# Layer 2's first upper product formed ahead from layer 1's sums and rows, with x2 made beside hop 1

## The chip, the cores and the metric

One Trainium2 chip, one core. The metric is the device time of one execution in microseconds (us), lower is better; several executions of a kernel are timed, and one more is profiled.

## The reference, cut to what matters

Four graph layers over N = 3327 nodes with 64 features and one dense-stored, sparsely filled adjacency matrix `adj`; each layer is added to its input and normalised. The change lies between layer 1 and layer 2:

```python
# layer 1: hyperbolic attention; m_i = sum_j v_ij * rows_j, then a chain of scalars per node,
# whose end is  x2 = layernorm(x1 + layer1(x1))
x = _layernorm(x + _L1_gnn_ref(x, adj, L1_gnn_att_W, L1_gnn_att_b), axis=-1)
# layer 2: two hops
for k in range(HOP):
    agg = adj @ x
    x = jnp.tanh(jnp.concatenate([agg, x], axis=1) @ W[k])
```

The concatenation makes each hop `tanh(adj @ (x @ W_top) + x @ W_bottom)`. For each node, x2 is a combination `alpha * m + beta * xc` of layer 1's sums m and of the centred input rows xc, with two scalars alpha and beta that come out of the chain.

## The kernel before, in words

Nodes are padded to 26 blocks of 128 (`NB`), which lie in pairs: a `[128, 26, 64]` tile holds one block's rows per slot, and the transposed form `[128, 1664]` stacks a pair's 64 features twice. Chunks of 416 columns (`CW`) cut the 1664 (`HALF`) into four. The adjacency is held transposed in HBM, one block of 128 rows being 1664 KB.

**Layer 1** (`near_sphere`, from L973) runs 104 tiles. For each: TensorE products (L1053), VectorE and ScalarE work (L1065, L1066, L1074), and sums of `v` over nodes on TensorE (`acc`, L1086). The four sums are copied to `mT` (L1094). `gather` is called for each tile in turn; after the third last tile TensorE takes six early products with `all_m` (L1264), and ScalarE reads them after the last but one (L1269, L1273). GpSimd multiplies mT and ljT for the sums of products `p` (L1259 for half of mT, L1277 for a quarter). Here `ljT[0]` holds layer 1's rows, transposed.

**`blocks_ahead`** (L1657) then opens the buffers for the adjacency blocks of layer 2 (`strm`, four of them; `late`, two), in memory that layer 1's tiles had, and issues their loads on SyncE (all by L209, in `block`): blocks 0 to 3 (`at_l`) and two that stay for both hops (`kept`, blocks 20 and 21). Blocks 22 to 25 have been kept since the start. SyncE's order is the planner's; those of TensorE, ScalarE and VectorE in these stages are written out by hand (`manual_schedule`), GpSimd's only in layer 1's loop.

**`near_end`** (L1286) is the chain of scalars, 26 per partition: three sums per node (`p`, `q` and the last feature `t`) from products with `all_m` (L1340) and `but_last` (L1350), some forty small VectorE operations with a tanh (L1392) and two roots by ScalarE (L1422, in `rsqrt2`, with one Newton step each), idle matmuls that keep TensorE awake (`awake`, L1326), and the centred weights of layer 3 (`centred_weights`, L301). Then x2 = al * m + bx, bx = be * xc: GpSimd (L1454) and ScalarE (L1457) make bx, VectorE the rest (L1463 to L1467).

**`layers`** (L309) begins with hop 1 (k = 0). `turned` transposes a group of x2 (L345, L349), `top` multiplies it by the upper weights and copies the product to `hw` = `lj` (L355, L391), `bottom` multiplies by the lower weights into the accumulators (L394), and `add` adds one adjacency block: 8 products of 128x416 by halves (L403). The order of the blocks is 0 to 3, 25, 4 to 7, 24, 8 to 11, 23, 12 to 15, 22, 16 to 19, and at the end 20 and 21 chunk by chunk (`chunk_end`, L475), with the tanh (L478). New blocks are loaded into `strm` (`at_l`) and `more` (`bt_l`, two buffers) as TensorE frees them. Hop 2 takes the same way, beginning with the last six blocks that hop 1 loaded; layer 3 follows.

Hop 1's head, in short, interleaves the making of hw with the first two blocks:

```python
turned(0); turned(1); top(0, nc.scalar.copy); turned(2); top(1)
for c in range(CPH): add(c, order[0])
turned(3); top(2); turned(4); top(3)
for c in range(CPH): add(c, order[1])
top(4)
for c in range(CPH): bottom(c)
```

Of the kernel before, what the change touches and what calls it, by code (L numbers as in the profile page):

```python
# [10 lines left out]
F32 = mybir.dt.float32  # L11
# [3 lines left out]
AF = mybir.ActivationFunctionType  # L15
# [8 lines left out]
D = 64  # L24
# [49 lines left out]
def kernel(  # L74
# [234 lines left out]
    def layers(ctx, x2, x3, kept, ready, ahead_ctx, strm):  # L309
# [67 lines left out]
        with tc.tile_pool(name="l2p", bufs=2, space=PSUM, reuse_waits="tile") as l2p:  # L377
            for k in range(2):
# [49 lines left out]
                if k == 0:  # L428
# [20 lines left out]
                else:  # L449
# [13 lines left out]
                for i, jb in enumerate(order):  # L463
# [6 lines left out]
                    for c in range(CPH):  # L470
                        add(c, jb)
                    if k and jb in held and len(held) == 2:
                        for q in range(AHEAD + 3):
                            masks(q)
# [384 lines left out]
    with tc.tile_pool(name="l1", bufs=1) as l1:  # L859

        def l1_stat(name):
            return l1.tile([P, NB], F32, name=name)

        aa, g1, ga, xn, rxn, gs, gs2, gk, lpn = (
            l1_stat(name) for name in ("aa", "g1", "ga", "xn", "rxn", "gs", "gs2", "gk", "lpn")
# [107 lines left out]
        def near_sphere(mT, xm, sq_e, t_e):  # L973
# [3 lines left out]
            with tc.tile_pool(name="n1", bufs=1, reuse_waits="tile") as n1, tc.tile_pool(  # L977
# [10 lines left out]
                ljT = [n1.tile([P, HALF], F32, name=f"ljT_{k}") for k in range(2)]  # L988
# [206 lines left out]
                with tc.manual_schedule(  # L1195
# [80 lines left out]
                    of = slice(2 * CW, 3 * CW)  # L1276
                    nc.gpsimd.tensor_tensor(xm[:, of], mT[:, of], ljT[0][:, of], ALU.mult)  # L1277
                    layer_3_constants()
# [5 lines left out]
                    vec(xn, aa, rxn, ALU.mult)  # L1284

        def near_end(mT, xm, sq_e, t_e, x2):  # L1286
# [3 lines left out]
            with tc.tile_pool(name="l1e", bufs=1) as l1e, tc.tile_pool(  # L1290
                name="l1t", bufs=1, space=PSUM
            ) as l1t, tc.tile_pool(name="l1m", bufs=5, space=PSUM) as l1m:

                prod = l1e.tile([P, NB, D], F32, name="prod_xm")
                sqm = l1e.tile([P, NB, D], F32, name="prod_mm")
# [14 lines left out]
                def both(a, scalar, b, tag, op0, op1):  # L1310
# [5 lines left out]
                    engines={mybir.EngineType.PE, mybir.EngineType.Activation, mybir.EngineType.DVE}  # L1316
                )
                in_order.__enter__()
                gss = of(mul, gs, s, "gss")
                gks = both(gk, -2.0, s, "gks", mul, mul)  # L1320
                aav = lin(aa, 1.0 / D, LN_EPS, "aav")
                idle = l1t.tile([P, 512], F32, name="idle_e")

                def awake(t):

                    nc.tensor.matmul(  # L1326
                        idle[:NB, :], t, xc[:, :8].rearrange("p n d -> p (n d)"),
                        start=True, stop=True,
                    )

                gt = st("gt")
                p, q = st("p"), st("q")
                nc.vector.tensor_reduce(q[:, :12], sq_e, axis=AX.X, op=add)
                pms = {}

                def both_products(g, n):

                    pm = l1m.tile([P, 3, P + 2], F32, tag="pm", name=f"pm_{g}")[:, :n]
                    for k in range(n):
                        nc.tensor.matmul(  # L1340
                            pm[:, k], mT[:, (g + k) * P : (g + k + 1) * P], all_m,
                            start=True, stop=True,
                        )
                    pms[g] = pm

                for g, n in threes[2:]:
                    both_products(g, n)
                pe = l1t.tile([P, 9, 2], F32, name="pe")
                for k in range(9):
                    nc.tensor.matmul(  # L1350
                        pe[:, k], xm[:, k * P : (k + 1) * P], but_last, start=True, stop=True
                    )
                for g, n in threes[:2]:
                    both_products(g, n)
                for g, n in threes[2:]:
                    m = pms[g][:, :, :P].rearrange("p n (h d) -> p n h d", h=2)
                    nc.scalar.activation(by_half(sqm)[:, g : g + n], m, AF.Square)
                    if g > 6:
                        vec(by_half(prod)[:, g : g + n], m, by_half(xc)[:, g : g + n], mul)
                vec(gt[:, :12], t_e, gk[:, :12], mul)  # L1360
                for g, n in threes[2:]:
                    sl = slice(2 * g, 2 * (g + n))
# [4 lines left out]
                nc.vector.tensor_reduce(p[:, 18:], prod[:, 18:], axis=AX.X, op=add)  # L1367
                nc.vector.tensor_reduce(q[:, 12:], sqm[:, 12:], axis=AX.X, op=add)
                nc.vector.tensor_copy(p[:, :18], pe.rearrange("p n h -> p (n h)"))

                k = of(mul, p, gks, "k")
                vec(k, k, gt, add)
                gp = of(mul, p, gss, "gp")
                vec(p, p, s, mul)
# [7 lines left out]
                awake(u2)  # L1382
                centred_weights(l1t)
# [6 lines left out]
                awake(th)  # L1390
                arg, th = th, st("tanh")
                nc.scalar.activation(th, arg, AF.Tanh, scale=-1.0)  # L1392
# [10 lines left out]
                al = of(mul, ca, gs, "al")  # L1403
                vec(be, be, ck, sub)
                alp = of(mul, al, p, "alp")
                bea = of(mul, be, aa, "bea")
                al2 = of(mul, al, al, "al2")
                n2 = both(alp, 2.0, bea, "n2", mul, add)
                vec(al2, al2, q, mul)
                vec(n2, n2, be, mul)  # L1410
                vec(alp, alp, bea, add)
                vec(n2, n2, al2, add)
                awake(n2)
                root = lin(n2, MIN_NORM * MIN_NORM, None, "root", ALU.max, ALU.bypass)
                dn = lin(y2, 1.0, None, "dn", add, ALU.bypass)
                stt(dn, uy, 2.0, dn, op0=mul, op1=add)
                sca(dn, dn, MIN_NORM, None, ALU.max)

                def rsqrt2(v, tag):

                    r0 = st(f"{tag}_r")
                    nc.scalar.activation(r0, v, AF.Sqrt)  # L1422
                    awake(v)
                    nc.vector.reciprocal(r0, r0)
                    t = of(mul, v, r0, f"{tag}_t")
                    vec(t, t, r0, mul)
                    stt(t, t, -3.0, r0, op0=add, op1=mul)
                    return t


                r0 = st("rdn")
                nc.vector.reciprocal(r0, dn)
                on = rsqrt2(root, "on")
                f = both(on, -0.5 * MAX_NORM, r0, "f", mul, ALU.min)
                vec(n2, n2, f, mul)
                vec(al, al, f, mul)
                stt(n2, alp, 2.0, n2, op0=mul, op1=add)
                vec(be, be, f, mul)
                vec(n2, n2, f, mul)
                sca(be, be, 1.0, None, add)  # L1440
                stt(n2, n2, 1.0 / D, aav, op0=mul, op1=add)
                vec(be, be, s, mul)
                r = rsqrt2(n2, "ln")
                stt(be, r, -0.5, be, op0=mul, op1=mul)
                stt(al, r, -0.5, al, op0=mul, op1=mul)
                awake(al)
                bx = l1e.tile([P, NB, D], F32, name="bx")
                rows = [slice(2 * g, 2 * (g + n)) for g, n in threes]

                def one(v, sl):  # L1450
# [279 lines left out]
```

## Time and profile before

| what | us |
|---|---|
| median of three runs | 568.14 (567.31 to 568.34) |
| the profiled execution | 566.58 |
| its span (first to last instruction) | 564.9 |
| TensorE busy in the span | 527.5 (93%) |
| VectorE, ScalarE, GpSimd busy | 362.7, 277.3, 216.7 |
| layer 1's last sum begins, in the span | 225.8 |
| first product of hop 1 with an adjacency block (L403) | 248.4 |
| hop 2's first product (L355) | 326.7 |

Time points are counted from the span's start. In the profile's rows PE is TensorE's matmuls, PEld its weight loads, DVE VectorE, ACT ScalarE, POOL GpSimd, SPq SyncE's queue, which issues loads; L403 is line 403 of the kernel before. A row of a timeline has start, length, engine, line, operation, what is written and read, and how many instructions were merged. The row of GB/s is one window in 40 equal slices. "DMA to landing" is the time from a load's issue until its semaphore tells that it is there.

### The profile page before, as it was taken

To read this page: it belongs to the slowest core of one execution; us is meant where nothing else is said; L and a number is where in the kernel's file an instruction comes from. 1 tells how busy PE (TensorE), PEld (TensorE's weight loads), DVE (VectorE), ACT (ScalarE), POOL (GpSimd) and SP (SyncE) were. 2 spreads that over 40 slices of the span, in tenths; PEclk is the share of its full clock that TensorE was granted. 3 is DMA by queue.
4 is the path that set the end of the run, shared out by engine and by line. 5 is a ranking of instruction groups with operands and counts; after the bars stand their busy time and mean duration, and the time that the engine had idled before them with its cause. 6 is when DMAs were issued, how large, how long until landed. Compare 5 with 4: busy or idle time off the path is not lost.

```text
span 564.9 us, 7457 instructions
## 1 busy us (share of the span) xinstructions
PE 527.5 (93%) x2827; PEld 221.9 (39%) x2827; DVE 362.7 (64%) x527; ACT 277.3 (49%) x330; POOL 216.7 (38%) x134
## 2 busy tenths in 40 slices
PE   8899989999999999779999999999999999999992
PEld 5523222222222223444444454443455555545542
DVE  6899999999999999750000010400378888787834
ACT  4899999999999997350000000000274333343311
POOL 3799999999999999110000000000011000000000
PEclk9899999999999999999999999999999999999997
DMA  8986766660576671999999219999609986689801
GB/s 293 356 282 202 237 201 219 208 231 0 188 236 203 222 238 35 386 430 424 427 426 424 113 49 411 425 426 382 243 0 307 359 303 244 214 267 338 302 2 36
DMA packets 34037, 145.27 MB, mean 257 GB/s; under 512 B 10285, under 2 KB 11975, under 8 KB 28871
## 3 DMA queue, kind: packets, MB, share of 16 engines
q1 hardware_dynamic: 31655, 144.11, 69.5%
q10 hardware_dynamic: 2336, 0.59, 0.5%
q8 instruction: 24, 0.39, 0.3%
q14 instruction: 22, 0.18, 0.1%
HBM read 143.23 MB, written 0.87 MB: 255 GB/s over the span
## 4 chain that ended last, share of the span: by engine, by line
PE 63%; DVE 20%; ACT 8%; issue 5%; DMA 2%; DVEq 0%; POOL 0%; POOLq 0%
PE cnt L403 23%; PE pq L1053 12%; DVE v L1074 12%; PE cnt L498 11%; PE acc L694 6%; ACT sg L1029 4%; PE acc L709 3%; ACT pq L1066 2%; DVE a L1065 2%; DMA at_l<-in_adjT 2%; PE pn_l L355 1%; DVE w L511 1%; PE cnt L394 1%; DVE mask L337 1%; PE idle L889 1%
## 5 line engine op out<-in xcount | busy, mean ns | idle before, releaser
L1040 POOL TENSOR_TENSOR u<-sg,at 128x832 f32<-128x832 f32 x88 | 169.8, 1960 | 3.2 <-ACT sg L1029 2.7
L1053 PE MATMUL pq<-riT,ljT 64*128 64x416 f32 x416 | 100.2, 560 | 15.2 <-DVE v L1074 6.3
L1065 DVE SCALAR_TENSOR_TENSOR a<-pq,dl,u 128x832 f32<-128x832 f32 x104 | 111.8, 1076 | 3.0 <-PE pq L1053 2.9
L1066 ACT ACTIVATE pq<-pq,al,gas 128x832 f32<-128x832 f32 x104 | 104.9, 1010 | 15.2 <-DVE a L1065 14.2
L1074 DVE SCALAR_TENSOR_TENSOR v<-pq,a 128x832 f32<-128x832 f32 x104 | 105.5, 1014 | 1.1 <-ACT pq L1066 0.7
L1086 PE MATMUL acc<-v,xv 128*64 128x416 f32 x416 | 95.4, 538 | 0.1
L1029 ACT ACTIVATE sg<-lb,rb 128x1664 f32<-128x1664 f32 (+1 forms) x53 | 87.3, 1647 | 0.1
L403 PE MATMUL cnt<-at_l,lj 128*64 128x416 f32 x480 | 86.3, 513 | 0.6 <-DMA at_l<-in_adjT 0.6
L513 ACT ACTIVATE w<-cnt 128x832 int16<-128x832 f32 x55 | 47.2, 863 | 71.5 <-PE cnt L498 71.4
L478 ACT ACTIVATE hT<-cnt 128x416 f32<-128x416 f32 x8 | 4.1, 517 | 148.6 <-PE cnt L403 148.6
L625 POOL TENSOR_TENSOR s<-sq,s 128x384 bf16<-128x384 f32 (+1 forms) x4 | 4.1, 1026 | 188.0 <-ACT s L624 188.0
L511 DVE TENSOR_SCALAR w<-cnt 128x832 int16<-128x832 f32 x49 | 50.1, 1023 | 25.8 <-PE cnt L498 24.5
L1053 PEld LDWEIGHTS pq<-riT,ljT 64*128 64x128 f32 x416 | 31.5, 184 | 88.3 <-DVE v L1074 83.0
L391 DVE COPY lj<-pn_l 128x384 f32<-128x384 f32 (+2 forms) x8 | 4.3, 541 | 85.2 <-PE pn_l L355 85.2
L403 PEld LDWEIGHTS cnt<-at_l,lj 128*64 128x64 f32 x480 | 34.0, 137 | 50.0 <-issue 47.7
L498 PE MATMUL cnt<-mask,tri 128*128 128x416 bf16 x208 | 53.5, 339 | 0.1
L694 PE MATMUL acc<-w,s 128*128 128x416 bf16 x208 | 52.6, 339 | 0.5 <-DVE hid L766 0.5
L498 PE MATMUL cnt<-mask,rest 128*128 128x416 bf16 x200 | 51.6, 340 | 1.2 <-ACT w L513 0.6
L1086 PEld LDWEIGHTS acc<-v,xv 128*64 128x64 f32 x416 | 20.6, 134 | 61.0 <-issue 57.7
L337 DVE TENSOR_SCALAR mask<-ah 128x1664 bf16<-128x1664 f32 x42 | 43.4, 1033 | 0.0
L403 PE MATMUL cnt<-kept,lj 128*64 128x416 f32 x192 | 35.5, 513 | 0.0
L1040 POOL TENSOR_TENSOR u<-sg,kept 128x832 f32<-128x832 f32 x16 | 30.9, 1962 | 3.8 <-ACT sg L1029 3.8
(283 smaller groups left out, 390.2 us busy)
## 6 DMA issues: line engine op xcount, KB each, us to landing
at_l<-in_adjT SPq DMA_DIRECT2D x26, 1664.0 KB, 12.0
at<-in_adjT SPq DMA_DIRECT2D x44, 832.0 KB, 4.9
ah<-in_adjT SPq DMA_DIRECT2D x42, 832.0 KB, 6.4
bt_l<-in_adjT SPq DMA_DIRECT2D x8, 1664.0 KB, 10.0
kept<-in_adjT SPq DMA_DIRECT2D x6, 1664.0 KB, 8.8
lb<-lf_rows SPq DMA_DIRECT2D x2, 384.0 KB, 4.4
ljT<-ljT SPq DMA_DIRECT2D x4, 128.0 KB, 6.4
x<-in_x ACTq DMA_DIRECT2D x1, 416.0 KB, 5.4
```

The lines of the kernel that those rows point to most:

```text
L337: nc.vector.tensor_scalar(mask[q], at, 0.0, None, ALU.not_equal)
L403: nc.tensor.matmul(acc[c][h * D : (h + 1) * D, :], hw[:, slot(jb), :], blocks[jb][:, o : o + CW], start=c not in begun, stop=last, skip_gr ...
L498: nc.tensor.matmul(cnt[c][:, e, :], mat, mask[q][:, of], start=start, stop=(mat is tri), skip_group_check=True,)
L511: nc.vector.tensor_scalar(w.bitcast(I16), cnt[c], 0.0, None, ALU.max)
L694: nc.tensor.matmul(acc[h, c][:, e, :], s12[:, slot(jb)].rearrange("p t d -> p (t d)"), ws[q, c][:, e, :], start=first, stop=last,)
L1029: nc.scalar.activation(sg[:, :, of], lbs[:, :, of], AF.Sigmoid, bias=rb[:, sl : sl + 1])
L1040: nc.gpsimd.tensor_tensor(u, sg[:, :, of], at[:, :, of], ALU.mult)
L1053: nc.tensor.matmul(pq[:, h, :], ljT[h != jb // NBH][rows, of], riT[rows, ch * CW : (ch + 1) * CW], start=True, stop=True,)
L1065: stt(a_s[t], pqs[t], dl[:, one], us.pop(t), op0=ALU.add, op1=ALU.mult)
L1066: nc.scalar.activation(pqs[t], pqs[t], AF.Square, bias=al[:, one], scale=gas[:, one])
L1074: stt(w, pqs.pop(t), CUBIC_REST, a_s.pop(t), op0=ALU.add, op1=ALU.mult)
L1086: nc.tensor.matmul(accs[cp, ci][h * D : (h + 1) * D, :], xv[:, slot(jb), :], w[:, h, :], start=(jb == order[0]), stop=(jb == order[-1]),)
```

## The change: what it does

- **near_sphere** takes a tile `p_e`: after the last but one of layer 1's tiles, TensorE also multiplies the first six blocks of xm by `but_last` (12 instructions), and ScalarE copies the result. GpSimd's third quarter of xm and `layer_3_constants` go from here; one scalar (`aav`) is made here. `ljT[0]` lives on through near_end.
- **near_end**: VectorE makes the last two quarters of xm. All of `p` comes from products with `but_last`. `w_x` and `w_m` are made by TensorE and ScalarE from layer 2's upper weights, so that `ljT * w_x` is xc times the upper weights and `mT * w_m` is m times them. The 13 products with x run while the chain of scalars runs, those with m near its end. The chain is rewritten: the projection's root has no Newton step and no separate reciprocal of the denominator. Then, group by group, VectorE forms lj = alpha * (m W) + beta * (xc W), which is hw. The idle matmuls go.
- **x2 itself** (alpha * m + beta * xc) is made by VectorE after this, from copies of m by ScalarE, beside hop 1.
- **Hop 1** begins with `add`; x2 is turned after the fourth and the fifth block, and multiplied by the lower weights after the sixth.

The diff, cut to its core:

```diff
-                if k == 0:
+                if k == 0 and not begun_here:
                     turned(0)
...
-                else:
+                elif k:
...
                     for c in range(CPH):
                         add(c, jb)
+                    if k == 0 and begun_here:
+                        if i == 3:
+                            turned(0)
+                            turned(1)
+                        if i == 4:
+                            turned(2)
+                            turned(3)
+                            turned(4)
+                        if i == 5:
+                            for c in range(CPH):
+                                bottom(c)
...
                             nc.scalar.copy(
                                 t_e.rearrange("p (a k h) -> p a k h", a=2, k=3), pm[..., P:]
                             )
-                    of = slice(2 * CW, 3 * CW)
-                    nc.gpsimd.tensor_tensor(xm[:, of], mT[:, of], ljT[0][:, of], ALU.mult)
-                    layer_3_constants()
+                            pe = n1q.tile([P, 2, 512], F32, tag="pq", name="pe_early")[:, 0, :12]
+                            for b in range(6):
+                                nc.tensor.matmul(
+                                    pe[:, 2 * b : 2 * b + 2], xm[:, b * P : (b + 1) * P], but_last,
+                                    start=True, stop=True,
+                                )
+                            nc.scalar.copy(p_e, pe)
...
+                x_times_m(2)
+                gss = of(mul, gs, s, "gss")
+                gks = both(gk, -2.0, s, "gks", mul, mul)
+                x_times_m(3)
+                m_and_t(6, 3)
+                m_and_t(9, 3)
+                m_and_t(12, 1)
+                p_of(6, 9)
+                p_of(9, NBH)
+                squares(6, 3)
+                squares(9, 3)
+                squares(12, 1)
+                nc.scalar.activation(w3_dg, w3_dg, AF.Copy, scale=float(2**27))
...
+                first = in_bank("first_w")
+                nc.tensor.transpose(first[:, :P], all_m[:, :P], ident)
+                nc.tensor.matmul(
+                    first[:, P : 2 * P], center, w2_dg[:, 0, :], start=True, stop=True
+                )
+                nc.tensor.matmul(first[:, 2 * P : 3 * P], center, w3_dg, start=True, stop=True)
...
+                nc.scalar.copy(all_mT, first[:, :P])
+                nc.scalar.activation(w_x, first[:, P : 2 * P], AF.Copy, scale=rows_63)
...
+                second = in_bank("second_w")
+                nc.tensor.matmul(second[:, :P], all_mT, w2_dg[:, 0, :], start=True, stop=True)
+                xs = [in_bank(f"x_w_{g}") for g, _ in fours[:2]]
...
+                times(xs[0], ljT, w_x, *fours[0])
+                times(xs[1], ljT, w_x, *fours[1])
                 nc.scalar.activation(th, arg, AF.Tanh, scale=-1.0)
...
+                root = both(n2, 1.0 / MAX_NORM**2, dn, "root", mul, ALU.max)
+                nc.scalar.copy(w_m, second[:, :P])
+                nc.scalar.copy(w3_dg, first[:, 2 * P : 3 * P])
...
+                r0, r = table_root(root, "on")
+                x_out(xs[0], *fours[0])
+                x_out(xs[1], *fours[1])
+                m_out(6, 3)
+                rest_x = in_bank("x_w_8")
+                times(rest_x, ljT, w_x, *fours[2])
+                m_and_t(0, 3)
+                last_x = in_bank("x_w_12")
+                times(last_x, ljT, w_x, *fours[3])
+                hv = of(mul, root, aav, "hv")
+                stt(hv, n2, 1.0 / D, hv, op0=mul, op1=add)
+                vec(r, root, r, mul)
+                vec(r, r, r0, add)
+                var = of(mul, r, alp, "var")
+                stt(var, var, 1.0 / D, hv, op0=mul, op1=add)
+                stt(be, r, 0.5, be, op0=mul, op1=add)
+                r0, t = table_root(var, "ln")
+                x_out(last_x, *fours[3])
+                x_out(rest_x, *fours[2])
+                mw = [in_bank(f"m_w_{g}") for g, _ in fours]
+                for (g, n), pt in zip(fours, mw):
+                    times(pt, mT, w_m, g, n)
+                m_out(9, 3)
+                m_and_t(3, 3)
+                for g, n in ((12, 1), (0, 3), (3, 3)):
+                    m_out(g, n)
...
+                stt(alpha, n_r, -0.5, al, op0=mul, op1=mul)
+                stt(beta, n_r, -0.5, be, op0=mul, op1=mul)
+                for b, g, n in ((0, 0, 1), (0, 1, 3), (3, 12, 1), (1, 4, 4), (2, 8, 4)):
+                    sl = slots(g, n)
+                    pt = mw[b].rearrange("p (n d) -> p n d", d=D)
+                    pt = pt[:, sl.start - 8 * b : sl.stop - 8 * b]
+                    vec(pt, pt, one(alpha, sl), mul)
+                    vec(lj[:, sl], lj[:, sl], one(beta, sl), mul)
+                    vec(lj[:, sl], lj[:, sl], pt, add)
+                for g, n in threes:
+                    sl = slots(g, n)
+                    vec(x2[:, sl], x2[:, sl], one(alpha, sl), mul)
+                    vec(xc[:, sl], xc[:, sl], one(beta, sl), mul)
+                    vec(x2[:, sl], x2[:, sl], xc[:, sl], add)
                 in_order.__exit__(None, None, None)
+                nc.gpsimd.tensor_copy(tri, tri_f)
+                nc.gpsimd.tensor_scalar(rest, tri_f, -1.0, -STEP, ALU.mult, ALU.add)
...
                     mT = n1m.tile([P, HALF], F32, name="mT")
+                    ljT_0 = n1m.tile([P, HALF], F32, name="ljT_0")
...
+                    near_sphere(mT, ljT_0, xm, sq_e, t_e, p_e)
                     blocks = blocks_ahead(arm)
-                    near_end(mT, xm, sq_e, t_e, x2)
-                layers(x2, xc, *blocks)
+                    near_end(mT, ljT_0, xm, sq_e, t_e, p_e, x2)
+                layers(x2, xc, True, *blocks)
```

Of the new functions, `m_and_t` is the former pair of products with `all_m` for a group of blocks (3 banks), `p_of` the products with `but_last`, `m_out` and `x_out` are ScalarE's copies out of a bank, `times` is one product of 128x128 for each block of a group, and `in_bank` takes one of four banks in turn.

## The prediction

> **What bounds the kernel now.** I read the page first: TensorE is busy 93% of the span and the DMA share stands at 9 through slices 16 to 21. Two resources are full in one stage, so I went to the stage that the change touches, layer 1's end and hop 1 of layer 2, and first to the chain of waits:
>
> ```profile
> 229.72 5.88 issue
> 235.60 0.27 ACT both_m L305
> ...
> 242.46 0.20 DVE e_be L1444
> ...
> 242.68 2.30 ACT bx L1457 x10
> ...
> 248.48 2.94 PE cnt L403 x16
> ...
> 259.62 67.19 PE cnt L403 x384
> ```
>
> Columns are start, length, what. From 226 to 248 the chain is small work on vectors; from 259.62 on, TensorE's products with adjacency blocks (L403) run 67 us without a wait. Read alone, this says that an earlier start of hop 1 is worth its full size. So I asked for the other resource: the DMA bandwidth from 232 to 312 us, and the window of the last block's issue (SyncE's issue; then the tile's issue-to-landing line), and when TensorE uses it:
>
> ```profile
> GB/s 388 413 419 426 439 433 433 423 446 433 426 426 426 426 421 419 426 426 426 426 426 426 426 426 426 428 406 426 426 426 426 426 426 426 433 426 428 413 426 426
> ```
>
> ```profile
> 301.71 0.33 SPq L209 DMA_DIRECT2D at_l<-in_adjT  x1
> ```
>
> ```profile
> DMA to landing us min/median/max: 15.7/15.7/15.7
> ```
>
> ```profile
> 315.46 5.76 PE L403 MATMUL cnt<-at_l,lj 128*64 128x416 f32 x32
> ```
>
> The bandwidth is flat at 426 GB/s for 80 us. The last block, jb 19, lands at 301.71 + 15.7 = 317.4. The x32 group is blocks 18 and 19, 2.79 us each, so TensorE takes up block 19 at 315.46 + 2.79 = 318.25: only 0.85 us after it landed. Hop 1 is **bound twice**, and the second bound lies 0.85 us behind the first. What starts the stream (SyncE's timeline, its waits in 205 to 232 us, and TensorE's timeline there):
>
> ```profile
> 223.26 0.37 SPq L209 DMA_DIRECT2D kept<-in_adjT  x1
> 227.55 1.77 SPq L209 DMA_DIRECT2D at_l<-in_adjT  x4
> 229.36 0.55 SPq L209 DMA_DIRECT2D kept<-in_adjT  x1
> ```
>
> ```profile
> SPq L209 <- PE acc L1086: 3.9, 1, 3.9
> ```
>
> ```profile
> 224.28 1.61 PE L1264 MATMUL pq_early<-all_m,mT 128*128 128x130 f32 x12
> 225.81 1.63 PE L1086 MATMUL acc<-v,xv 128*64 128x416 f32 x8
> ```
>
> The first at_l issue waits 3.9 us, and the releaser is layer 1's last sum (L1086, ending 225.81 + 1.63 = 227.44), because the blocks lie where layer 1's tiles were. One block (issued 223.26) went ahead; its data run out near 229, and the bandwidth dips to about 107 GB/s there: the stream already starts with a hole.
>
> **What the Trainium skill says.** "DMA: Bandwidth & Descriptors", section "Anatomy of one DMA — SWDGE (gpsimd) path", says that DMA engines wait on no semaphore; the wait is on the issuing sequencer. The SyncE row agrees: 3.9 us of wait, then four issues at once. Its "Specifications" give a fabric ceiling of 435 GB/s; the trace has 426, so the stream cannot be hurried. "PSUM — Partial Sum Buffer", "Engine vs sequencer instructions", says matmuls start and complete in program order; the two PE rows above agree (the sums follow pq_early at once). "TensorE: Matmul & The Clock Gate", "Part 1: The HAM clock gate", says that about 3.4 us of idleness halves the clock; here gaps up to 1.6 us (L1326) left it at 1.00 in every 5 us stage from 229 to 254, so the removed idle matmuls (awake) and new gaps of that size cost nothing.
>
> **Part by part.**
>
> *p_e in the main loop.* Six more products (12 instructions) are put on TensorE behind the sums of the last tile but one and ahead of the last sums. Like instructions (pe, L1350, x18 in 2.07 us) start every 112 ns: 12 x 0.112 = **1.34 us**. Their inputs are there (GpSimd's xm ends 223.19 + 1.96 = 225.15), and v of the last tile ends at 226.47, just when TensorE becomes free, so nothing covers them. Queued behind: the last four sums, and on ScalarE the copies of mT (L1094), behind the p_e copy. The last sum ends at 228.8 in place of 227.44. Who waits for it: SyncE's first at_l issue, 227.55 to 228.9.
>
> *Products, sums and squares up to the first step of the scalars (e_ka, now 233.16).* GpSimd's 1.07 us product goes; VectorE gets two of 128x416 (0.59 each, as L558), of which the second waits for the later mT copy: 229.4 to 230.0. Then a reduction of 0.94, seven small ones (0.7), reductions of 0.5 and 0.67, and four small ones bring ka to about 233.2; the 1.34 us are paid back by what leaves VectorE: its wait for GpSimd's product (1.29) and the products with xc and their sums (0.74, 0.67). TensorE: 7 blocks of m (14 x 0.112) and 7 of p (14 x 0.112) end near 232.2, just before. I take 0, between -0.3 and +0.6.
>
> *Scalar chain.* Tanh sat 0.98 us behind e_th (234.78 to 235.76), because the both_m copy stood ahead on ScalarE; the copies now there (all_mT, w_x, 0.27 each) depend on products done near 233, so -0.75. From tanh's end to the first root 22 operations in place of 18, each 0.10 to 0.21: +0.35. From that root to the second one, 2.88 us (238.31 to 241.19) become 1 reciprocal and 7 operations, 1.70: -1.18. ScalarE's three copies between the roots (0.6 + 0.6 + 0.48) just fit. The second root comes near 239.5, alpha and beta near 241.1, against 242.75: **-1.6 us**.
>
> *Start of hop 1.* Gone: the bx rows (L1454, L1457), the sums into x2, nine transposes with copies, and the node products between them. In: TensorE runs 13 products with x and 13 with m (0.22 each), the x ones while the scalars run. Those with m stand behind m_and_t(0), which needs the bank that m_out(6) frees, so they run from about 240.6 to 244.2, and m_and_t(3) to 245.0. VectorE scales block 0 (three operations, 0.7) well before, then stays ahead of TensorE's 2.79 per block. First product about 245.6, with one bank's copy (0.5), in place of 248.41: -2.8.
>
> *Inside hop 1.* Between 248.41 and 259.62 TensorE did two blocks (5.58) and 5.63 of other things; now 13 transposes and 8 bottoms, 1.8 + 2.79 = 4.6: -1.0. x2's 15 operations (6.4 us) end on VectorE near 254, before turned(0) after the fourth block (256.7).
>
> Sum for **TensorE alone: -3.8**, so it would reach block 19 at 314.4.
>
> *Small ones.* Scaling w3 and making tri and rest move (0.3 to 0.5 us each on idle engines; first use of tri is after 408). SyncE's next issues (bt_l, 246.41) wait for tiles of layer 1's end, then for hop 1's blocks; all come sooner, and the stream is backed up to 252, so nothing starves it.
>
> *What is late next.* The stream. Its issue is 1.34 us later behind an existing hole, with nothing in it to absorb this: block 19 lands at 317.4 + 1.34 = 318.74. TensorE, there at 314.4, waits (some 4 us in pieces before blocks 14 to 19) and takes it up at 318.77 in place of 318.25: **+0.5 us**. Behind it come one block and the two kept ones, as before, and hop 2 issues its loads as TensorE frees buffers, so it moves along unchanged.
>
> The profiled execution took 566.58 us (span 564.9, 1.7 around it) and becomes about 567.1. The median of the runs is 568.14, 1.56 above it; the same +0.5 gives 568.7. The bound of the unknown: the delay is 1.2 at least if some of the hole absorbs it, and 1.6 with a restart; the slack in the timed runs lies between 0 and 0.9. So +0.3 to +1.6.
>
> **Rivals.**
> 1. *The issue isn't delayed* (the waiting tile is another one in the new layout). Then block 19 lands at 317.4, and the gain is the slack: 568.14 - 0.85 = 567.3. For it: tiles moved between pools. Against: v, which the last sum reads, is still among the last tiles below the blocks.
> 2. *The hole closes*: the scheduler puts the second kept block ahead of at_l, so that data flow from 223.3 on. The dip (about 0.9 us of full bandwidth) and the half-filled start (0.7) are won: landing at 315.8, gain 2.4, 565.7. Against: that block's place wasn't free at 223.6 before.
> 3. *Slower*: the 0.85 us of slack belong to the profiled run, the fastest here. In the timed ones, 1.56 longer, the stream may already end the hop; then the whole 1.34 comes through at the wait for block 19: 569.5. It decides once the true slack is under 0.2 us.
> 4. *TensorE's gain counts in full*, 564.3, needs a stream that ends 3 us sooner; nothing in the diff does that. I give it to rival 2's chance.
>
> **How the numbers follow.** What can be told from no change is about 0.2%, 1.14 us: 567.0 to 569.28. Forecast (568.4 to 569.2) 0.58, rival 1 0.12, rivals 2 and 4 0.10, rival 3 0.20. Faster: 0.10 and a sixth of rival 1, 0.12. Slower: 0.20 and a tail of the forecast, 0.22. Same: 0.66. The range leaves out rivals 2 and 4 and small tails: 566.9 to 569.8.
>
> **What would show it.** Right: the first at_l issue near 228.9 with releaser acc; block 19 landing near 318.7; TensorE waiting for at_l or bt_l in hop 1 (none now), some 4 us; first L403 near 245.6; the next hop's start within 1 us of 326.7. Wrong: the first issue near 227.5 or before, no waits of L403 on DMA in hop 1, or L403 starting after 249.

## The result, and the profile after

The changed kernel takes **572.19 us** (four executions, 571.8 to 574.4); the kernel before, timed beside it, 568.19 (567.31 to 568.34). The ratio of all executions is 1.0082, 95% interval 1.0053 to 1.011. So it is slower by 4.0 us by the medians and by 4.7 us by the ratio, where 0.5 had been forecast. The profiled execution took 574.4 us, with a span of 572.66; it is the slowest of the four, so its profile shows more loss than the median has.

The chain of waits from 222 us on, of the changed kernel (columns: start, length, what):

```profile
224.81 0.92 PE acc L1102 x4
225.73 1.54 PE pq_early L1280 x12
228.12 1.43 PE pe_early L1294 x12
239.11 0.96 ACT lj L1473 x2
240.50 0.94 PE pm L1363 x6
241.66 2.92 PE m_w L1467 x26
244.60 18.34 DMA bt_l<-in_adjT
262.98 3.01 PE cnt L403 x16
266.00 2.99 PE cnt L394 x8
268.99 2.97 PE cnt L403 x16
271.97 18.96 DMA bt_l<-in_adjT
290.98 11.42 PE cnt L403 x64
302.42 20.49 DMA at_l<-in_adjT
322.95 8.60 PE cnt L403 x48
```

Before, 67 us of products with blocks ran in this place without a wait. Now three transfers of 18 to 20 us stand between them: hop 1 is bound by the stream. The last line but one is block 19, issued at 302.42 and landing at 322.91, 5.5 us later than before (317.39). Of this, 1.4 us come from an earlier stage of this execution (below); 4.1 us remain. TensorE's waits in hop 1 (244 to 332 us; us in total, times, longest) say the same; before there was none for a block:

```profile
PE cnt L403 <- DMA at_l<-in_adjT: 3.4, 5, 1.0
PE cnt L403 <- DMA bt_l<-in_adjT: 2.2, 3, 1.0
```

And yet TensorE came to hop 1 earlier, as forecast (245.6 predicted, 248.41 before), in its timeline:

```profile
245.81 11.39 PE L403 MATMUL cnt<-at_l,lj 128*64 128x416 f32 x64 [0.57 <-ACT x L1373]
```

The bandwidth once the stream runs is the old one (40 slices of 232 to 312 us). So the transfers are not slower; they began later:

```profile
GB/s 280 419 428 439 426 433 433 439 426 428 417 419 426 426 426 426 426 426 426 426 426 426 426 421 419 426 426 426 426 426 426 426 426 426 426 421 419 426 426 426
```

What started it, first SyncE's timeline, then its waits from 205 to 235 us:

```profile
230.52 2.19 SPq L209 DMA_DIRECT2D at_l<-in_adjT  x4
232.81 0.92 SPq L209 DMA_DIRECT2D kept<-in_adjT  x2
```

```profile
SPq L209 <- PE acc L1102: 20.7, 1, 20.7
```

Before, kept block 20 was issued at 223.26 and filled the time until the four at_l could go. Now SyncE waits 20.7 us for layer 1's last sum with its first issue, and **both kept blocks stand behind it in its queue**. The stretches of 3 us show the hole (columns: stretch, length, busy time of each engine, TensorE's clock, DMA share, GB/s):

```profile
223.00:226.00 3.00, 2.89 (x15) 0.92 (x16) 3.00 (x4) 1.24 (x2) 3.00 (x2) 1.00 0.00 0
226.00:229.00 3.00, 3.00 (x25) 2.23 (x23) 2.44 (x8) 1.67 (x3) 0.53 (x1) 1.00 0.00 0
229.00:232.00 3.00, 3.00 (x23) 2.33 (x24) 1.78 (x5) 1.58 (x4) 0.00 (x0) 1.00 0.26 53
```

In the second of these stretches the kernel before moved 404 GB/s:

```profile
226.00:229.00 3.00, 3.00 (x22) 1.83 (x21) 1.64 (x10) 2.29 (x5) 1.60 (x3) 1.00 0.95 404
```

The diff has no line on SyncE; its order is the planner's, and it came out differently.

Two smaller things differ as well. TensorE's twelve early products delayed the last sums as expected:

```profile
228.05 1.50 PE L1294 MATMUL pe_early<-but_last,x 128*128 128x2 f32 x12
229.48 0.92 PE L1102 MATMUL acc<-v,xv 128*64 128x416 f32 x4
```

And this execution's layer 1 began 1.37 us later (first sum at 26.63, before 25.26), and TensorE's clock was halved from 12.5 to 19.4 us, in the kernel before only from 13.9 to 17.3. That is not the change: kernel `b_more_pe` below, which differs from the kernel before only near 238 us, has both too (first sum at 26.73, half clock from 12.8 to 19.7).

### The profile page after: what moved, and what is told of

The parts are those of the page before. It is cut to its first block, busy times and chain, and to the rows that moved or that the text cites. A ratio compares the mean times of both kernels' runs of the same rounds, so it can differ in the third digit from the quotient of the medians.

```text
span 572.7 us, 7513 instructions
## 1 busy us (share of the span) xinstructions
PE 529.0 (92%) x2854; PEld 225.6 (39%) x2854; DVE 369.1 (64%) x542; ACT 278.5 (49%) x329; POOL 213.4 (37%) x130
## 4 chain that ended last, share of the span: by engine, by line
PE 52%; DVE 21%; DMA 13%; ACT 8%; issue 3%; POOL 1%; DVEq 0%; POOLq 0%
PE cnt L403 15%; DVE v L1090 12%; PE pq L1069 12%; PE cnt L513 11%; DMA bt_l<-in_adjT 7%; DMA at_l<-in_adjT 6%; PE acc L709 6%; ACT sg L1045 4%; PE acc L724 3%; ACT pq L1082 2%; DVE a L1081 2%; DVE w L526 1%; PE cnt L394 1%; DVE mask L337 1%; DMA x<-in_x 1%
## 5 line engine op out<-in xcount | busy, mean ns | idle before, releaser
L391 DVE COPY lj<-pn_l 128x512 f32<-128x512 f32 (+1 forms) x4 | 2.4, 592 | 82.4 <-PE pn_l L355 82.4
```

## The experiments

A table first, from the traces (us from the span's start; "hop 2 to last" is from the start of hop 2's first product to the start of TensorE's last, "tail" from there to the span's end). The ratios are to the kernel before, timed on the same chip.

| kernel | first sum | first at_l issued | block 19 lands | hop 2 starts | hop 2 to last | tail | median | ratio (95%) |
|---|---|---|---|---|---|---|---|---|
| before | 25.26 | 227.55 | 317.39 | 326.74 | 227.94 | 10.18 | 567.8 to 568.2 | |
| after | 26.63 | 230.52 | 322.91 | 331.48 | 229.33 | 11.85 | 572.19 | 1.0082 (1.0053 to 1.011) |
| a_kept_first | 25.23 | 229.06 | 317.43 | 326.01 | 229.04 | 11.55 | 568.21 | 1.0011 (1.0000 to 1.0021) |
| a_pe_late | 26.59 | 228.94 | 321.21 | 329.79 | 228.44 | 11.56 | 571.47 | 1.0063 (1.0046 to 1.0081) |
| a_both | 25.66 | 227.93 | 317.10 | 325.68 | 228.58 | 11.72 | 568.91 | 1.0019 (1.0007 to 1.0031) |
| b_ljt_moved | 25.28 | 227.59 | 319.98 | 328.55 | 227.91 | 10.10 | 568.55 | 1.0014 (1.0002 to 1.0026) |
| b_pe_early | 25.20 | 229.06 | 318.74 | 329.76 | 227.95 | 9.78 | 569.25 | 1.0022 (1.0011 to 1.0034) |
| b_more_pe | 26.73 | 229.03 | 318.68 | 329.80 | 229.27 | 10.11 | 568.17 | 1.0006 (0.9991 to 1.0021) |
| a_end | 25.87 | 229.76 | 318.11 | 326.69 | 228.44 | 10.38 | 567.40 | 0.9989 (0.9976 to 1.0001) |
| a_end_pe | 25.74 | 229.57 | 317.88 | 326.46 | 228.66 | 10.51 | 567.34 | 0.9992 (0.9975 to 1.0010) |
| a_light | 26.53 | 230.36 | 314.55 | 325.04 | 228.46 | 11.31 | 566.09 | 0.9961 (0.9943 to 0.9978) |
| b_light | 25.36 | 227.69 | 312.77 | 326.89 | 228.24 | 11.19 | 568.71 | 1.0018 (1.0004 to 1.0032) |
| a_two_first | 25.72 | 229.54 | 315.85 | 324.43 | 228.37 | 9.96 | 565.34 | 0.9952 (0.9935 to 0.9970) |
| a_best | 25.37 | 227.57 | 317.24 | 325.82 | 228.47 | 10.04 | 566.93 | 0.9981 (0.9968 to 0.9995) |

Names with a_ are made from the changed kernel, those with b_ from the kernel before. The executions of one kernel that enter the ratios spread by up to 5 us, so a single profile shows where time lies, and the ratios how much. A difference of two ratios carries the uncertainty of both; it is given with "±" where it matters.

**a_kept_first: only the order of SyncE's issues is put back.**

```diff
-            for jb in range(UNDER_WAY):
-                ready[jb] = block(strm, jb, tag="at", name=f"at_l2_0_{jb}")
-            for jb in range(NB - EARLY - LATE, NB - EARLY):
-                all_kept[jb] = block(late, jb, name=f"kept_{jb}")
+            with tc.manual_schedule(engines={mybir.EngineType.SP}):
+                for jb in (20, 0, 1, 2, 3, 21):
...
```

> The kernel after, with one thing put back: SyncE issues kept block 20 ahead of blocks 0 to 3, as in the kernel before. Theory (the stream of blocks sets hop 1's end; it lost the head start of one block, 4.0 us of transfer): kept 20 is issued within 1 us of the last GpSimd product with adjacency, the last block lands 4.0 us sooner against the first at_l issue, and the time is 572.2 - 4.0 = 568.2, so within 0.5 us of the kernel before. Rival (the chain of scalars, the copies or a colder TensorE made layer 1's end longer): no change from 572.2. Rival (the start of the program, where the two profiles differ by 1.4 us, is what became slower): no change, and the offset stands before 222 us in the trace.

Measured: 568.21. SyncE's timeline has the old pattern again:

```profile
223.21 0.37 SPq L209 DMA_DIRECT2D kept<-in_adjT  x1
229.06 2.19 SPq L209 DMA_DIRECT2D at_l<-in_adjT  x4
```

The ratio falls from 1.0082 to 1.0011. The order alone is worth 0.71%, **4.0 us** (± 1.7), most of the loss of 4.7; what is left, 0.11% or 0.6 us, is close to the forecast (but see the program's end, below). Block 19 lands at 317.43, where the kernel before has it, although at_l was issued 1.5 us later.

**a_pe_late: the twelve products and their copy behind the last sums, in the planner's order.** The diff moves the six matmuls and `nc.scalar.copy(p_e, pe)` eight columns to the left, out of the branch that stands ahead of the sums.

> The kernel after, with the twelve early products of p (and the copy of them) put behind layer 1's last sums. Theory (the stream's first issue waits for the last sums, which these products delay): the first at_l issue comes 1.4 to 1.5 us sooner after the last v of layer 1, and the time falls by as much, 572.2 - 1.5 = 570.7. Rival (the scalar chain sets the end): p_e now comes later in that chain, so no gain, or a loss of up to 0.5.

Measured: 571.47, ratio 1.0063, so this edit brings 0.19%, 1.1 us (± 1.9): the timing can't tell it from nothing, nor from the forecast 1.5. The traces show the delay itself. Counted from layer 1's first sum, the first at_l is issued 1.5 us sooner than in the changed kernel, and block 19 lands 1.7 sooner. Here nothing lies ahead of at_l, and in these profiles its delay reaches the stream's end in full.

**a_both: the two together.**

> The kernel after with both edits: kept block 20 issued ahead, and the early products of p behind the last sums. Theory: the stream runs as in the kernel before, so the last block lands as there, and what is left is the slack that the kernel before had in front of its last block: 567.3, that is 0.9 us faster than before. TensorE still waits for blocks in hop 1, as its own path is some 3 us shorter than the stream. Rival (hop 1 bound by TensorE or by layer 1's end): 572.2 unchanged, or a gain of 3 us and more below the kernel before with no waits for blocks.

Measured: 568.91, a miss. Hop 2 starts 1.06 us sooner than in the kernel before, but the end comes later. In the table the loss stands in two other columns: 0.6 more from hop 2 to the last product and 1.5 more in the tail. That made the next question. It is also no better than a_kept_first (568.21). TensorE's clock halved in this execution during the chain of scalars, from 240.1 to 243.5 us, and the first product with a block came 220.8 us after layer 1's first sum, in the changed kernel 219.2 (TensorE's clock is the last column but two):

```profile
236.00:240.00 4.00, 1.73 (x13) 1.45 (x13) 3.34 (x27) 2.93 (x9) 0.00 (x0) 1.00 1.01 429
240.00:244.00 4.00, 4.00 (x24) 4.00 (x23) 2.05 (x11) 1.69 (x5) 0.00 (x0) 0.57 1.01 433
```

**b_ljt_moved: what turned the order over?** In the kernel before, `ljT[0]` alone is held on through near_end, as the change does.

```diff
                     mT = n1m.tile([P, HALF], F32, name="mT")
+                    ljT_0 = n1m.tile([P, HALF], F32, name="ljT_0")
```

> The kernel before with one part of the change alone: ljT_0 is held in the pool that lives on through near_end, and nothing uses it there. By the compiled program the planner then puts blocks 0 to 3 ahead of kept 20 on SyncE. Theory: the stream has a block more to move after the last sums, 4.0 us, of which the slack of 0.85 us before the last block takes up its part: 568.2 + 3.1 = 571.3, with TensorE waiting for blocks at hop 1's end. Rival (the memory's place makes no difference, the new chain is to blame): 568.2, no change.

SyncE's order turns over with this one tile:

```profile
227.59 2.15 SPq L209 DMA_DIRECT2D at_l<-in_adjT  x4
229.84 0.90 SPq L209 DMA_DIRECT2D kept<-in_adjT  x2
```

So a buffer's move is enough; why the planner then chooses so is not settled. In this profile block 19 landed 2.6 us later, TensorE waited 1.5 us for blocks and hop 2 began 1.8 later. The timing shows less than was expected: 568.55, 0.14% or 0.8 us (0.1 to 1.5), where 3.1 were forecast. A late stream should cost the kernel before less than the changed one, as its TensorE comes to block 19 some 4 us later; but the forecast had counted that, so the size of the miss is not explained. A part of it may be the profile that the forecast started from: it is 1.6 us below the median, and its stream lost 0.9 us underway, which this one's did not.

**b_pe_early: the twelve products ahead of the last sums in the kernel before, their result unused.**

```diff
+                            pe = n1q.tile([P, 2, 512], F32, tag="pq", name="pe_early")[:, 0, :12]
+                            for b in range(6):
+                                nc.tensor.matmul(
+                                    pe[:, 2 * b : 2 * b + 2], xm[:, b * P : (b + 1) * P], but_last,
...
+                            nc.scalar.copy(p_e, pe)
```

> The kernel before with the twelve early products with but_last and their copy added ahead of layer 1's last sums, their result unused; the rest is untouched. The step of the prediction (nothing in the stream absorbs the delay) has the first at_l issue 1.3 us later and block 19 landing as much later, so +0.5 us after the slack: 568.5. The theory from the runs so far (the tail of the kept block that was sent ahead covers the delay): the issue comes 1.3 us later, but the kept block is still landing then, so block 19 lands within 0.4 us of 317.4 and the time is unchanged, 568.0, ratio 0.999 to 1.001.

Measured: 569.25, ratio 1.0022 (1.25 us), so neither. The issue came 1.51 us later, the first at_l landed 1.0 later and block 19 1.35 later:

```profile
223.20 0.37 SPq L209 DMA_DIRECT2D kept<-in_adjT  x1
229.06 2.24 SPq L209 DMA_DIRECT2D at_l<-in_adjT  x4
```

The tail of the kept block covers only 0.5 of the delay, so the revised theory falls and the prediction's step ("nothing in it to absorb this") was nearly right. That block 19 lands at 318.74, to the digit as forecast, is luck: 1.0 of the delay came through at the start, and 0.4 came underway. What made a_kept_first's block 19 punctual is something else: in its stream, blocks land 4.00 us apart from first to last, while the streams of before, b_pe_early and b_more_pe each lose 0.6 to 1.3 us at one or two points (0.9 between 300 and 309 us in the kernel before). One profile of each cannot say whether that belongs to the kernel or to the execution; the cause stays open. Both expectations also forgot that the chain of scalars starts 1.5 us later here and nothing pays it back, so that TensorE comes to hop 1 later. It waited for no block in hop 1, so in this kernel the loss is TensorE's own. In this execution its clock fell too, just where hop 1 begins:

```profile
249.00:251.00 2.00, 2.00 (x11) 1.78 (x9) 0.00 (x0) 0.96 (x2) 0.00 (x0) 0.50 1.01 426
251.00:253.00 2.00, 2.00 (x11) 0.92 (x12) 0.56 (x1) 0.00 (x0) 0.00 (x0) 0.77 1.00 426
```

The kernel before had 1.00 in both stretches.

**a_end: the program's end.** a_kept_first with six loads added in an arm that isn't taken, so that SyncE's later code moves and nothing more is executed.

```diff
+            for _ in range(6):
+                nc.sync.dma_start(attb_sb, att_b.partition_broadcast(P))
```

> The changed kernel with kept block 20 issued first, plus six small loads on SyncE in an arm of the program that is not taken, so that SyncE's code after that arm lies further on; no work is added to what is executed. Theory: the 1.5 us at the program's end are a program fetch in SyncE's closing instructions; moved, they vanish, and the time falls from 568.2 to 566.7, the stretch from the last layer-3 sum to the end from 14.9 to 13.5 us. Rival (the end is longer for what the change did to layer 3 or to the final stores): no change, 568.2.

Measured: 567.40, and the tail falls from 11.55 to 10.38. In the DMA view of the last 7 to 8 us (queue, kind: packets, MB, share), first a_kept_first, then a_end:

```profile
q14 instruction: 7, 0.06, 2.1%
```

```profile
q14 instruction: 6, 0.05, 2.5%
```

One fetch of program code of 8192 bytes fewer. In the trace of a_kept_first SyncE's second closing semaphore instruction comes 2.0 us after the first, and in a_end 0.08. So the longer end is a matter of where SyncE's code lies; that its closing instructions straddled a piece that had to be fetched is the reading that fits the pause and the extra fetch. In time it is 0.22%, 1.25 us (± 0.9). b_light below, whose SyncE code is two loads shorter than that of before, gets the longer tail the other way round (11.19).

**b_more_pe and a_end_pe: TensorE's program fetch in hop 2.** In hop 2 a fetch of 16384 bytes fell at 64.5 to 65.1 us after its start in the four changed kernels above, within the last block's transfer; at 48.7 and 70.1 in the kernel before. The first kernel adds 14 tiny products to the kernel before, the second 24 to a_end:

```diff
+                for _ in range(14):
+                    nc.tensor.matmul(idle[:2, :2], but_last, but_last, start=True, stop=True)
```

> The kernel before with 14 tiny products more (some 60 instructions) on TensorE where it idles in the chain of scalars, nothing else. Theory of the program fetch: TensorE's program is fetched in pieces of fixed size, and its place in hop 2 moves with the number of instructions ahead of it; here the fetch at about 70 us after hop 2's start moves to about 65, into the transfer of hop 2's last block, which then lands 0.5 to 1.3 us later, and TensorE waits so much longer for it: 568.5 to 569.3. Rival (the fetch is harmless, the late landing in the changed kernels has another cause): no change, 568.0.

> As the kernel with SyncE's code moved, plus 24 tiny products on TensorE during the chain of scalars, which move TensorE's program fetch of hop 2 about 9 us ahead, out of the last block's transfer. Theory: hop 2's last block lands 0.5 to 1.0 us sooner after hop 2's start, so 566.0 if both fetches matter. If only the end's matters, 566.7; if neither, 568.2.

In b_more_pe's trace it came out as expected: the fetch moved to 65.3, the last block landed 70.24 us after hop 2's start (before 68.94), and hop 2 to last grew from 227.94 to 229.27. TensorE's timeline, first before, then b_more_pe:

```profile
395.72 3.01 PE L403 MATMUL cnt<-at_l,lj 128*64 128x416 f32 x16 [0.59 <-DMA at_l<-in_adjT]
```

```profile
400.09 1.97 PE L403 MATMUL cnt<-at_l,lj 128*64 128x416 f32 x10 [1.75 <-DMA at_l<-in_adjT]
```

But the time (568.17, interval -0.5 to +1.2 us) doesn't show it, and a_end_pe speaks against the simple form. There the fetch moved to 57.2, the block before the last landed 0.7 us later than usual (61.64), the last one at 69.64 (a_end 69.40), and the time was 567.34, like a_end's. All fourteen traces agree in one thing: in the eight with a fetch at 64.4 to 65.3 the last block landed 0.4 to 1.3 us late against the 4.00 us per block, and in the other six not at all. So such a fetch goes with a late block; no timing here shows a cost, and the rule is open.

**a_light and b_light: the stream made shorter.** Both replace two loads of hop 1 by a block that is there.

```diff
                 blocks = {**ready, **kept}
+                if k == 0:
+                    order = [24 if jb in (8, 9) else jb for jb in order]
```

> The changed kernel with the loads of blocks 8 and 9 left out of hop 1, where TensorE multiplies by the kept block 24 in their place: as many products, two loads (some 8 us of the stream) fewer; hop 1's sums leave out blocks 8 and 9. Theory: without the stream's bound TensorE's own gain shows: no waits for blocks, hop 2 starts 3.8 us sooner than in the kernel before (322.9); with the 1.5 us at the program's end and 0.7 in hop 2 that stay, 566.4, ratio to the kernel before 0.997. Rival (TensorE gained less than the prediction's sum): hop 2 starts at 325 or later and the time is 568 or more.

> The kernel before with the same two loads left out (hop 1's sums leave out blocks 8 and 9). Theory: TensorE bounds its hop 1, so hop 2 starts near 326.7 as before and the time stays at 568.0. Rival (the stream already bounds it in most executions): 567 or less.

The changed kernel gains 1.21% by it (1.0082 to 0.9961, 6.9 us), the kernel before nothing: it even takes 0.18% more, and its tail is 1.0 us longer. So the stream bounds hop 1 in the changed kernel, and TensorE does in the kernel before. The size of TensorE's own gain can be read here. From layer 1's first sum to hop 2's start a_light needs 325.04 - 26.53 = 298.51 us, the kernel before 326.74 - 25.26 = 301.48: 2.97 less. It still waits 0.8 us for blocks:

```profile
PE cnt L403 <- DMA bt_l<-in_adjT: 0.5, 1, 0.5
PE cnt L403 <- DMA at_l<-in_adjT: 0.3, 1, 0.3
```

2.97 + 0.8 = **3.8 us**, the sum of the prediction for TensorE alone. (Hop 2 starts at 325.04 and not at the 322.9 expected, for these 0.8 us and because layer 1 began 1.3 us later in this execution.) The two parts of that sum are not as forecast, though: the first product with a block comes 219.1 us after layer 1's first sum, before 223.2, and from there hop 1 takes 79.4 us with the waits, before 78.3.

**a_two_first: both kept blocks ahead.** a_end with the order 20, 21, 0, 1, 2, 3.

> The changed kernel with SyncE's closing code moved, and with both kept blocks (20 and 21) issued ahead of the four at_l. If the second one's place is free at 224 too, the stream has no hole: 3.3 us of data more are sent before at_l's places come free, block 19 lands 1.5 to 2.5 us sooner than with one kept block first, hop 2 starts near 324, and the time is 565.5. Rival (its place comes free only with layer 1's last sum): nothing changes, 567.4, or the at_l issues come later and it is 568.

Measured: 565.34, as the theory said; ratio 0.9952, **2.7 us faster than the kernel before**, of which the moved closing code is worth 1.25. The second kept block's place was free at once:

```profile
223.69 0.84 SPq L209 DMA_DIRECT2D kept<-in_adjT  x2
229.54 1.77 SPq L209 DMA_DIRECT2D at_l<-in_adjT  x4
```

From 226 us on the stream has no hole any more:

```profile
226.00:229.00 3.00, 3.00 (x23) 1.93 (x22) 1.65 (x7) 1.24 (x4) 0.00 (x0) 1.00 0.94 399
229.00:232.00 3.00, 3.00 (x28) 2.63 (x24) 2.73 (x13) 2.06 (x6) 0.00 (x0) 1.00 1.03 439
```

Against a_end it is 0.37%, 2.1 us (± 1.2). TensorE's gain comes through here, since the stream's end moved with it: block 19 lands at 315.85 and hop 2 starts at 324.43.

**a_best: a_both, the moved end, and 56 tiny products to shift the fetch.** It joins the edits of a_both and a_end with two groups of 28 products like those above, where TensorE idles in the chain.

> The changed kernel with kept block 20 first, the twelve early products behind the last sums, SyncE's closing code moved, and 56 tiny products on TensorE where it idles in the chain of scalars, so that its program fetch falls some 15 us ahead in hop 2, near 50 us after its start. Theory: hop 2 starts 1 us sooner than before, its last block lands 69.0 after that in place of 69.6, the end is 13.5: 566.5 to 567.0. If the fetches don't matter: 568.0.

Measured: 566.93, ratio 0.9981, in the expected range, but not by the expected way: the last block landed at 69.45, with fetches at 45.6 and 66.8 and not near 50. It isn't the best one; a_two_first is.

## Why the prediction was wrong, by its own steps

- **"Its issue is 1.34 us later behind an existing hole … block 19 lands at 317.4 + 1.34 = 318.74."** This is the step that failed. It takes for granted that kept block 20 still goes ahead of at_l: SyncE's order was taken over from the kernel before, and only a better one was considered (rival 2). The planner put at_l first, and the stream lost what kept block 20 had sent between 223 and 229 us: block 19 landed 4.1 us later, counted from layer 1's first sum. Putting it back takes 4.0 us off the time, and the kernel then stands at 568.21, half a us under the 568.7 forecast. That it comes so close is in part luck, since the program's end, for which the forecast had no term, adds 1.25 of it. The sentence above, that SyncE's order is the planner's, was the warning.
- **p_e, "12 x 0.112 = 1.34"**: right. The row is 1.50 us long; the last sums begin 1.43 after its start; at_l was issued 1.51 later in b_pe_early, the same edit alone.
- **"nothing in it to absorb this"**: off by about 0.5 us. In b_pe_early the first block landed 1.0 later for an issue 1.5 later. (The dip in the stream of the kernel before is to 173 GB/s from 229 to 230 us, not to 107; by the same windows of 1 us, 228 to 232 lost an estimated 1.1 us of full bandwidth, where rival 2 counts 0.9.)
- **The chain of scalars**: right. Tanh waits no more behind a copy (236.07, right after e_th), and the two roots are 1.63 us apart (240.51 - 238.88), predicted 1.70, before 2.88. Alpha and beta are there 2.0 us sooner after layer 1's first sum, where 1.6 was forecast.
- **First product 245.6**: measured 245.81, though layer 1's sums ended at 230.40 in that execution and not at 228.8. From there it is 15.4 us, where 16.8 was counted: 0.4 less up to ka (at 234.41), 1.0 less after it. So the close agreement is luck: a later start of layer 1 hides that the gain up to here, from layer 1's first sum, is 4.0 us and not 2.8.
- **TensorE alone, -3.8**: the sum is right, by a_light, but its two terms are not, and their errors cancel. The first product comes 4.0 us sooner and not 2.8; within hop 1 nothing is gained (0.3 lost, without the waits), where -1.0 was forecast for the transposes and products that moved into it. **Hop 1 bound twice**: right, by a_light and b_light.
- **The slack of 0.85 us before block 19**: the size was uncertain in a way the prediction did not see. That stream held one irregular delay of 0.9 us (its blocks else land 4.00 apart), so by this estimate an execution without it would have twice the slack.
- **Hop 2 "moves along unchanged", and no term for the program's end**: failed in small terms. The tail grew by 1.4 to 1.7 us in the changed kernels that keep SyncE's code where it is (1.25 in the timing), and hop 2 by 0.5 to 1.4 in single profiles. Nothing in the diff touches either. For the tail, a_end shows that the place of the code does it; for hop 2, b_more_pe's profile points the same way and its timing doesn't show it.
- **Removed idle matmuls "cost nothing"**: open, and the reason given for it fell. The size of TensorE's gaps did not decide: in the same stretch of the chain (240 to 244 us) the clock was 1.00 in after and 0.57 in a_both, with almost the same work and the same longest gap (1.3 us). The Trainium skill, "TensorE: Matmul & The Clock Gate", section "Part 1: The HAM clock gate", says that the clock depends on activity in a free-running window; chance in where the window falls would fit this, and each stretch of half clock in or after the chain lasted 3.4 us. It came within the chain in a_kept_first, a_both and a_best. But it came too, just after the chain, in b_pe_early and b_more_pe, which keep the idle matmuls, so no run shows that their removal is to blame.

Rival 2 named the right place. Its price was good too: it put block 19 at 315.8 and the time at 565.7, and a_two_first, which makes that order by hand, has 315.85 and 565.34, with the tail kept as short as before by the moved code. But the argument against it, "that block's place wasn't free at 223.6", was a wrong reading of a queue: in the kernel before, the second kept block stood behind four at_l that waited, and its issue tells nothing of when its place came free. (In the changed kernel it was free at 224; in the kernel before no run tried it.) And the same planner that could improve the order could spoil it; that case had no price. Rival 3 ended on the right side by another mechanism: in it the stream came 1.34 us late, not 4.1, and its premise, a stream that already bounds hop 1 in the kernel before, is not borne out by b_light.

## What to carry to other kernels

Where the order of a queue is made by a planner, a change that has no line on that queue can still turn it over, here by the move of one tile. So forecast the order, not only the waits, and price the case that the head start is lost: the first issue of a full stream is worth its own size at the stream's end. An issue that stands behind a waiting one shows when the queue let it go, not when its buffer was free; ask which transfers could pass the one that waits. And a gain on one of two bounds this near to each other pays only if the other moves with it: the same change costs 4.7 us (by the ratio) with one order of six loads and brings 2.7 with another, 1.25 of which are the closing code's.

## What the runs showed of the hardware that was not expected

- Code is fetched by DMA while the program runs, in pieces of 16384 and 8192 bytes. With one fetch more, and a pause of 2.0 us between two of SyncE's closing instructions, the end is 1.2 us later (a_end against a_kept_first: tail 10.38 and 11.55, fetches 6 and 7).
- A fetch of some 1.1 us on one queue, at 64.4 to 65.3 us in hop 2, went with a last block 0.4 to 1.3 us late in eight traces (1.2 in b_more_pe); other fetches of the same length, as at 302.7 us in after, left the blocks' distance at 4.00 us.
- A block of 1664 KB lands every 4.00 us over 20 blocks, to within 0.05 us (a_kept_first, a_end, after), which is 426 GB/s. This makes a delay of a few tenths readable in a single trace.
- TensorE's clock can halve without a long gap: it did so for 3.4 us in a_both, a_kept_first, b_pe_early and b_more_pe after 3.4 us in which TensorE was busy 1.4 to 1.8 us and no gap was over 1.4 us. With the same gaps it stayed at 1.00 in after. In a_best it halved although tiny products filled the gaps (none over 0.4 us).
